# Moving small work between engines in a four-layer convolution stack: broadcast columns, pooling sums, replicas and a rectifier

## The chip, the cores and the metric

One core of a Trainium2 chip runs the whole kernel in one launch. The metric is the device time of that launch in microseconds. The engines are named as in the profile: PE (TensorE; PEld is its weight load), DVE (VectorE), ACT (ScalarE), POOL (GpSimd) and SP (SyncE, which issues all DMAs here).

## The reference

The input x is (32, 128, 56, 56) in float32: 32 images, 128 channels, 56 x 56 points (L = 3136). Four residual layers follow each other, `x = x + layer(_gn(x))`, where `_gn` is a group norm with 32 groups of 4 channels.

```python
# layer 0: mixes 4 expert matrices by attention on the pooled input, then dilated depthwise convs
attn = softmax((relu(pooled @ fc1_w.T + fc1_b) @ fc2_w.T + fc2_b) / 34.0)
y    = einsum(agg(attn, dw_weight), x) + attn @ dw_bias
out  = sum(silu(depthwise3x3(y, ds_weight, dilation=d) + ds_bias) for d in (1, 3, 5))
# layer 1: a cubic B-spline of every element, 10 coefficients
# layer 2: linear attention; q and k come from x pooled to 8 x 8 cells (7 x 7 points each)
out  = depthwise3x3(linear_attention(relu(pool @ Wq.T + bq), relu(pool @ Wk.T + bk), Wv x + bv))
# layer 3: mamba over the 3136 points, 256 inner channels, 16 states each
xn   = layer_norm_over_channels(x)
xc   = silu(conv_b + causal_conv4(in_proj_x(xn)));  z = in_proj_z(xn)
dt, B, C = split(x_proj(xc))
delta = softplus(dt_proj(dt) + dt_proj_b)
h[t] = exp(delta[t] * A) * h[t-1] + delta[t] * B[t] * xc[t]
out  = out_proj((sum_n h[t, n] * C[t, n] + xc * D) * silu(z))
```

## The kernel before

Channels are partitions, points are the free axis. An image is cut into 7 chunks of 448 points (8 rows of 56). The kernel runs layer 3 of image b while layers 1 and 2 of image b + 1 and layer 0 of image b + 2 run beside it. The program has a part before the first scan (the first images' early layers), a hardware loop over 30 images that is unrolled by 6, and two images after it.

The layer-3 scan sets the beat. A chunk has 16 steps (`STEPS`), 3584 over all images. One step covers 32 channels x 4 states in the 128 partitions, twice, as one row of 904 elements:

- ACT makes the decays, `da = exp(A * delta)`, from `rep`, in two ops; PE spreads the rows of B over the partitions into the PSUM tile `pb`.
- DVE multiplies, `db = rep * pb` (into PSUM), and runs the scan, `h = scan(da, db)` (three buffers of h).
- POOL saves the last column (`last`) and multiplies by the rows of C, `hc = h * cb`; `cb` is a copy that ACT makes from PSUM into one of four buffers of the pool `cbp`.
- PE sums `hc` over the states into `y`.

`rep` holds delta and du = delta * xc, copied to all state groups. For that `ssm_inputs` writes both to DRAM (`flat`), and `fetch` reads them back with four different partition groups as targets.

In `ssm_inputs` softplus is made as max(v, 0) + ln(1 + exp(-|v|)), where v = dt_proj(dt) + bias: ACT writes |v| into `du` from PSUM, DVE writes max(v, 0) into `delta` from the same PSUM tile, ACT applies Exp and Ln to `du`, and POOL adds. `layer_norm` of the next chunk has its ops there too: PE centres (`ctr`) into a PSUM tile, ACT squares it (`sq`) and copies it (`cen`), PE averages, ACT makes `rstd`, POOL multiplies cen by it.

All matmul targets but `pb`, `db2` and `y` share one pool of four PSUM tiles (`mm`). `group_stats` makes the group norm's mean and rstd with a chain of ops on one element per partition: `mv`, `mg`, `dm`, `vv`, `ve`, `rs` (the last on POOL). `linear_attention` sums x over the 8 x 8 cells: first over the 7 points of a row into 448 sums (`s1`, in the tile `ws`), then over 7 rows (`s2`).

The order of all this isn't the order of the code. A planner (`Plan`) records every operation with the tiles it reads and writes, prices it (`price`), and gives it a due time counted back from its step (4 us each); to that it adds a fitted date from the table `LEAD`, by engine, output and input:

```python
for w in self.works:
    w.due += LEAD.get(w.what, 0.0)
```

It then builds the order greedily with its own clock: of an engine's operations that could start first it takes the one with the earliest due time, and it counts pool tiles as taken until their last reader. The instructions are issued in that order, so almost all of them bear the one line of `issue` (L456) in the profile, and are told apart by their tiles.

Of the kernel before, what the change touches and what calls it, by code (L numbers as in the profile page):

```python
# [37 lines left out]
KEXP = 4  # L38
# [42 lines left out]
    "gpsimd delta delta": -3.5,  # L81
    "gpsimd du delta": -20,
    "gpsimd hc h": 10,
    "gpsimd ind xt": -2.5,
    "gpsimd last h": -8.5,
    "gpsimd rep": 11.5,
    "gpsimd rep last": 8,
    "gpsimd rs ve": -87,
    "gpsimd rstd cen": -144,
    "gpsimd xn": -27,  # L90
    "gpsimd xn rstd": -55,
    "gpsimd xn xn": 3.5,
    "gpsimd xt xt": 4.5,
    "scalar aggT dwT": -0.5,
    "scalar att att": 3,
    "scalar cb mm": 0.5,
    "scalar cen mm": -1,
    "scalar da rep": 13,
    "scalar dbl mm": -20.5,
    "scalar du du": -12.5,  # L100
    "scalar du mm": -65,
    "scalar hats hats": -2,
    "scalar hats stack": 2.5,
    "scalar rstd mm": -67.5,
    "scalar rstd rstd": 1.5,
    "scalar sq mm": -17.5,
    "scalar top ab": -6.5,
    "scalar ws mm": -3.5,
    "scalar yc mm": -33,
    "sync flat delta": 15,  # L110
    "sync flat du": 7.5,
    "sync flatx xt": -114.5,
    "sync out_dram xt": 30,
    "sync padded yc": 17,
    "sync rep flat": 42,
    "sync stack flatx": -8,
    "sync stack padded": -10.5,
    "sync xt x_dram": -58,
    "tensor mm aggT": 5.5,
    "tensor mm cbT": -6.5,  # L120
    "tensor mm ctr": 2,
    "tensor mm dsT": 1.5,
    "tensor mm dtT": -5.5,
    "tensor mm fc1T": -1,
    "tensor mm gmat": -21,
    "tensor mm hid": 12,
    "tensor mm ident": -15,
    "tensor mm jmat": -1,
    "tensor mm outT": -1,
    "tensor mm winT": 1.5,  # L130
    "tensor mm wpT": -50,
    "tensor mm wqT": -1.5,
    "tensor mm ws": 6,
    "tensor mm wspl": -11,
    "tensor mm wv": 4,
    "tensor mm xprojT": -2,
    "tensor y ddiag": 4,
    "vector ab mg": 4,
    "vector ab rs": -27.5,
    "vector ab ve": 1.5,  # L140
    "vector aggT dwT": -80.5,
    "vector aggb aggb": 30.5,
    "vector aggb attb": 23,
    "vector att att": -33,
    "vector att mm": -9,
    "vector attb att": -56.5,
    "vector attr att": -93.5,
    "vector bia bia": 1.5,
    "vector bia kneg": -23,
    "vector cb mm": -4.5,  # L150
    "vector ctr ident": -36.5,
    "vector cube sq": 6,
    "vector db rep": 21,
    "vector delta mm": -10,
    "vector dm mv": -6.5,
    "vector g t": 12,
    "vector h da": -4.5,
    "vector hid mm": -1,
    "vector kb mm": 18,
    "vector mcell mg": 25,  # L160
    "vector mg mm": 14,
    "vector mv st": 5.5,
    "vector mx att": -10,
    "vector mx mx": -6.5,
    "vector nm": 13.5,
    "vector nm mg": 13.5,
    "vector pooled dm": 3.5,
    "vector rden mm": 4.5,
    "vector rden rden": 0.5,
    "vector scl mm": -4.5,  # L170
    "vector sz sz": -11,
    "vector sz t": 3,
    "vector ve mm": 4,
    "vector vv dm": 1.5,
    "vector ws": 5,
    "vector ws mm": 1.5,
    "vector ws ws": 6.5,
    "vector ws xt": -36.5,
    "vector xt mm": 19,
    "vector xt xt": 6,  # L180
# [21 lines left out]
class Plan:  # L202
# [6 lines left out]
    RATE, LANDING = 2e5, 1.8  # L209
# [64 lines left out]
    def price(self, w, engine, method, args, kw):  # L274

        n = args[0].free_size()
        if method == "dma_start":
            w.cost += 0.4 if bass.MemoryType.DRAM in (args[0].space, args[1].space) else 0.6
# [202 lines left out]
def tile_conv_stack(ctx: ExitStack, tc: tile.TileContext, out: bass.AP, x: bass.AP, w: dict):  # L481
# [14 lines left out]
    cbp = pool("cbp", 4)  # L496
# [192 lines left out]
    flats = [dramp.tile([2, DI * P * CH], F32, name=f"flat{k}") for k in range(2)]  # L689
# [14 lines left out]
    plan.pitch |= {fl[:].tensor.name: DI * P * CH for fl in flats}  # L704
# [20 lines left out]
    def group_stats(st):  # L725
# [10 lines left out]
        nc.vector.scalar_tensor_tensor(vv[:], dm[:], dm[:, 0:1], mv[:, 1:2], ALU.mult, ALU.add)  # L736
# [56 lines left out]
    def dynamic_conv(xt, st):  # L793
# [18 lines left out]
        nc.vector.tensor_scalar(att[:], att[:], mx[:, 0:1], 1.0 / TEMP, ALU.subtract, ALU.mult)  # L812
        nc.scalar.activation(att[:], att[:], AF.Exp)
        nc.vector.tensor_reduce(mx[:], att[:], AX.X, ALU.add)
        nc.vector.reciprocal(mx[:], mx[:])
        nc.vector.tensor_scalar_mul(att[:], att[:], mx[:, 0:1])
# [3 lines left out]
        nc.vector.tensor_scalar_mul(attr[:], att[:], rs[:, 0:1])  # L820
# [144 lines left out]
    def linear_attention(xt, st):  # L965
# [17 lines left out]
        nc.vector.tensor_reduce(s1, xt[:].rearrange("p (a b) -> p a b", b=W // GRID), AX.X, ALU.add)  # L983
# [7 lines left out]
        nc.vector.tensor_scalar(s2, s2, mcell[:, 0:1], rs[:, 0:1], ALU.subtract, ALU.mult)  # L991
# [134 lines left out]
    def ssm_inputs(xt, k, norm):  # L1126
# [30 lines left out]
        for t, src in enumerate((delta, du)):  # L1157
            nc.sync.dma_start(flats[k % 2][t : t + 1, :].rearrange("a (d p c) -> p (a d) c", d=DI, p=P), src[:])
# [371 lines left out]
```

## Time and profile before

| | us |
|---|---|
| median of 3 runs | 14950.99 (14941.11 to 14951.97) |
| the profiled execution | 14946.83 |
| its span, first to last instruction | 14945.0 |
| DVE / POOL / ACT busy | 13958.2 / 11265.0 / 10743.3 |
| PE busy (modelled ends) | 13091.0 |
| mean granted PE clock | 0.942 |

The lines of the groups give, for an engine, an operation and its tiles: the count, the busy time, the mean of one in ns, the engine's idle time before them and what ended it. The windows view gives the busy time of each engine in a stretch of the span.

### The profile page before, as it was taken

To read this page: it belongs to the slowest core of one execution; us is meant where nothing else is said; L and a number is where in the kernel's file an instruction comes from. 1 tells how busy PE (TensorE), PEld (TensorE's weight loads), DVE (VectorE), ACT (ScalarE), POOL (GpSimd) and SP (SyncE) were. 2 spreads that over 40 slices of the span, in tenths; PEclk is the share of its full clock that TensorE was granted. 3 is DMA by queue.
4 is the path that set the end of the run, shared out by engine and by line. 5 is a ranking of instruction groups with operands and counts; after the bars stand their busy time and mean duration, and the time that the engine had idled before them with its cause. 6 is when DMAs were issued, how large, how long until landed. Compare 5 with 4: busy or idle time off the path is not lost. (4 is left out here: it accounts for less than half of the span.)

```text
span 14945.0 us, 207438 instructions
## 1 busy us (share of the span) xinstructions
PE 13091.0 (88%) x68640; PEld 4525.0 (30%) x68640; DVE 13958.2 (93%) x13510; ACT 10743.3 (72%) x17159; POOL 11265.0 (75%) x9926
## 2 busy tenths in 40 slices
PE   6888898888898888988888988889988889888887
PEld 2323333323333233333333332333332333333222
DVE  2899999999999999999999999999999999999899
ACT  3777677777777776777777777767777777777664
POOL 2777777777778777777777777777877777777776
PEclk8999999999999999999999999999999999999998
DMA  6666676666676666666666666667666667666543
GB/s 160 145 155 159 151 164 158 148 152 154 156 159 154 155 152 148 161 158 150 156 158 150 157 153 154 156 150 162 159 151 150 155 151 168 153 152 159 134 105 71
DMA packets 1326438, 2257.40 MB, mean 151 GB/s; under 512 B 143222, under 2 KB 951545, under 8 KB 1324667
## 3 DMA queue, kind: packets, MB, share of 16 engines
q1 hardware_dynamic: 1325338, 2243.87, 65.1%
q8 instruction: 553, 9.06, 0.3%
q14 instruction: 547, 4.47, 0.1%
HBM read 1813.23 MB, written 430.08 MB: 150 GB/s over the span
## 5 line engine op out<-in xcount | busy, mean ns | idle before, releaser
L456 POOL TENSOR_TENSOR hc<-h,cb 128x896 f32<-128x896 f32 x3584 | 7498.9, 2096 | 782.0 <-PE y L456 395.7
L456 DVE TENSOR_TENSOR_SCAN h<-da,db 128x904 f32<-128x904 f32 x3584 | 7279.8, 2031 | 176.8 <-ACT da L456 8.4
L456 ACT ACTIVATE da<-rep,alog 128x448 f32<-128x448 f32 x7168 | 4432.7, 663 | 2275.2 <-DVE h L456 1922.3
L456 DVE TENSOR_TENSOR db<-rep,pb 128x904 f32<-128x904 f32 x3584 | 3940.2, 1099 | 196.7 <-PE pb L456 85.5
L456 PE MATMUL pb<-dbl,sel 128*128 128x452 f32 x3584 | 1954.3, 629 | 674.5 <-DVE db L456 645.1
L456 POOL COPY last<-h 128x2 f32<-128x2 f32 x3072 | 575.6, 189 | 2308.5 <-DVE h L456 2059.2
L456 PE MATMUL y<-hc,ids 128*32 128x448 f32 x14336 | 1962.7, 573 | 177.3 <-POOL hc L456 114.3
L456 PE MATMUL mm<-stack,dsT 96*32 96x448 f32 (+1 forms) x16128 | 1819.0, 562 | 44.7 <-DMA stack<-onesd 21.2
L456 PE MATMUL mm<-xn,winT 128*128 128x448 f32 x3584 | 1619.4, 572 | 122.4 <-DVE g L456 49.7
L456 ACT ACTIVATE hats<-stack,bia 128x448 f32<-128x448 f32 x2688 | 1638.4, 663 | 4.1 <-DMA stack<-flatx 3.6
L456 PE MATMUL mm<-hats,wspl 128*32 128x448 f32 x12544 | 1423.8, 579 | 91.1 <-DVE xt L456 52.7
L456 ACT ACTIVATE hats<-hats,one,scl 128x1344 f32<-128x1344 f32 x896 | 1347.7, 1504 | 1.2
L456 ACT ACTIVATE t<-mm 128x448 f32<-128x448 f32 x1568 | 837.4, 537 | 615.9 <-PE mm L456 549.0
L456 PEld LDWEIGHTS pb<-dbl,sel 128*128 128x128 f32 x3584 | 592.3, 199 | 1828.0 <-DVE db L456 1491.6
L456 PE MATMUL mm<-dbl,sel 128*128 128x448 f32 x1792 | 883.8, 584 | 112.6 <-DVE delta L456 48.1
L456 POOL TENSOR_TENSOR xt<-xt,g 128x448 f32<-128x448 f32 x672 | 766.0, 1140 | 270.8 <-DVE g L456 239.1
L456 PEld LDWEIGHTS mm<-xn,winT 128*128 128x128 f32 x3584 | 665.7, 196 | 887.7 <-issue 718.2
L456 PEld LDWEIGHTS mm<-stack,dsT 96*32 96x32 f32 (+1 forms) x16128 | 446.4, 111 | 1227.2 <-issue 1014.0
L456 PEld LDWEIGHTS y<-hc,ids 128*32 128x32 f32 x14336 | 371.5, 111 | 1395.2 <-issue 543.0
L456 PEld LDWEIGHTS mm<-hats,wspl 128*32 128x32 f32 x12544 | 379.8, 116 | 1087.7 <-issue 664.8
L456 ACT ACT_TABLE_LOAD x512 | 656.9, 1283 | 8.7
L456 ACT COPY cb<-mm 128x448 f32<-128x448 f32 x896 | 470.3, 526 | 232.5 <-POOL hc L456 112.1
(186 smaller groups left out, 15286.5 us busy)
## 6 DMA issues: line engine op xcount, KB each, us to landing
rep<-flat SPq DMA_DIRECT2D x3584, 224.0 KB
stack<-padded SPq DMA_DIRECT2D x2688, 264.0 KB
stack<-flatx SPq DMA_DIRECT2D x896, 224.0 KB
flat<-delta SPq DMA_DIRECT2D x224, 448.0 KB
flat<-du SPq DMA_DIRECT2D x224, 448.0 KB
padded<-yc SPq DMA_DIRECT2D x224, 264.0 KB
padded<-yc SPq DMA_DIRECT2D x256, 231.0 KB
xt<-x_dram SPq DMA_DIRECT2D x224, 224.0 KB
```

The source lines that it names most:

```text
L456: call()
```

## The change

- In `group_stats`, the softmax of `dynamic_conv` and the cells of `linear_attention`, DVE ops that take a per-partition scalar column become ops of two tensors, with the column broadcast along the free axis. `vv` and the normalising of the cells become two ops each; the softmax's factor 1/TEMP moves into ACT's Exp.
- The first pooling sum (7 points of a row) becomes six additions on POOL.
- `delta`, max(v, 0), is made by ACT's Relu with the bias column.
- `flat` is laid out so that a fetch takes four transfers of 8 x 448 rows per partition, not eight of 4 x 448.
- `cbp` gets a fifth buffer, the planner's price of a DMA and its bandwidth figure change (no DMA here reaches the size of the new price), and the table `LEAD` is new throughout.

```diff
 LEAD = {
...
-    "gpsimd hc h": 10,
+    "gpsimd hc h": 10.5,
...
+    "gpsimd ws ws": 13,
+    "gpsimd ws xt": -4.5,
...
-    "scalar cen mm": -1,
+    "scalar cen mm": 172,
...
+    "scalar delta mm": -2,
...
-    "sync rep flat": 42,
+    "sync rep flat": 61,
...
-    "vector h da": -4.5,
+    "vector h da": -76,
...
-    RATE, LANDING = 2e5, 1.8
+    RATE, LANDING = 2.4e5, 1.8
...
-            w.cost += 0.4 if bass.MemoryType.DRAM in (args[0].space, args[1].space) else 0.6
+            w.cost += 0.4 if args[0].partition_size() * n < P * P * 32 else 1.0
...
-    cbp = pool("cbp", 4)
+    cbp = pool("cbp", 5)
...
-    flats = [dramp.tile([2, DI * P * CH], F32, name=f"flat{k}") for k in range(2)]
+    flats = [dramp.tile([DI, 2 * P * CH], F32, name=f"flat{k}") for k in range(2)]
...
-        nc.vector.scalar_tensor_tensor(vv[:], dm[:], dm[:, 0:1], mv[:, 1:2], ALU.mult, ALU.add)
+        nc.vector.tensor_mul(vv[:], dm[:], dm[:])
+        nc.vector.tensor_add(vv[:], vv[:], mv[:, 1:2])
...
-        nc.vector.tensor_scalar(att[:], att[:], mx[:, 0:1], 1.0 / TEMP, ALU.subtract, ALU.mult)
-        nc.scalar.activation(att[:], att[:], AF.Exp)
+        nc.vector.tensor_sub(att[:], att[:], mx[:].to_broadcast([P, KEXP]))
+        nc.scalar.activation(att[:], att[:], AF.Exp, scale=1.0 / TEMP)
...
-        nc.vector.tensor_scalar_mul(att[:], att[:], mx[:, 0:1])
+        nc.vector.tensor_mul(att[:], att[:], mx[:].to_broadcast([P, KEXP]))
...
-        nc.vector.tensor_scalar_mul(attr[:], att[:], rs[:, 0:1])
+        nc.vector.tensor_mul(attr[:], att[:], rs[:].to_broadcast([P, KEXP]))
...
-        nc.vector.tensor_reduce(s1, xt[:].rearrange("p (a b) -> p a b", b=W // GRID), AX.X, ALU.add)
+        cells = xt[:].rearrange("p (a b) -> p a b", b=W // GRID)
+        nc.gpsimd.tensor_add(s1, cells[:, :, 0], cells[:, :, 1])
+        for i in range(2, W // GRID):
+            nc.gpsimd.tensor_add(s1, s1, cells[:, :, i])
...
-        nc.vector.tensor_scalar(s2, s2, mcell[:, 0:1], rs[:, 0:1], ALU.subtract, ALU.mult)
+        nc.vector.tensor_sub(s2, s2, mcell[:].to_broadcast([P, P2]))
+        nc.vector.tensor_mul(s2, s2, rs[:].to_broadcast([P, P2]))
...
-            nc.vector.tensor_scalar(delta[:, db, :], ps, dtb[:, db : db + 1], 0.0, ALU.add, ALU.max)
+            nc.scalar.activation(delta[:, db, :], ps, AF.Relu, bias=dtb[:, db : db + 1])
...
-            nc.sync.dma_start(flats[k % 2][t : t + 1, :].rearrange("a (d p c) -> p (a d) c", d=DI, p=P), src[:])
+            half = flats[k % 2][:, t * P * CH : (t + 1) * P * CH]
+            nc.sync.dma_start(half.rearrange("d (p c) -> p d c", p=P), src[:])
...
-        flat = flats[k % 2][:, db * P * CH : (db + 1) * P * CH].rearrange("t (r q c) -> q t r c", r=NS, q=Q)
+        flat = flats[k % 2][db : db + 1, :].rearrange("a (r q c) -> q (a r) c", q=Q, c=CH)
...
-                for t in range(2):
-                    nc.sync.dma_start(reps[db][Q * s : Q * s + Q, t, :, NGRP:], flat[:, t, :, :])
+                rows = reps[db][Q * s : Q * s + Q].rearrange("p t r c -> p (t r) c")
+                nc.sync.dma_start(rows[:, :, NGRP:], flat)
```

More of the change, by code (lines that the diff above doesn't have):

```diff
@@ L80 @@
 LEAD = {
-    "gpsimd delta delta": -3.5,
-    "gpsimd du delta": -20,
-    "gpsimd hc h": 10,
[L84 to L96, printed above, removed]
-    "scalar cen mm": -1,
-    "scalar da rep": 13,
-    "scalar dbl mm": -20.5,
@@ L100 @@
[L100 to L114, printed above, removed]
-    "sync rep flat": 42,
-    "sync stack flatx": -8,
-    "sync stack padded": -10.5,
@@ L118 @@
[L118 to L121, printed above, removed]
-    "tensor mm dsT": 1.5,
[L123 to L133, printed above, removed]
-    "tensor mm wspl": -11,
-    "tensor mm wv": 4,
-    "tensor mm xprojT": -2,
@@ L137 @@
[L137 to L154, printed above, removed]
@@ L155 @@
-    "vector dm mv": -6.5,
-    "vector g t": 12,
-    "vector h da": -4.5,
[L158 to L180, printed above, removed]
+    "gpsimd delta delta": 5.5,
+    "gpsimd du delta": -35,
+    "gpsimd hc h": 10.5,
+    "gpsimd ind xt": -6,
+    "gpsimd last h": -11.5,
+    "gpsimd rep": 60.5,
+    "gpsimd rep last": 25.5,
+    "gpsimd rs ve": 10,
+    "gpsimd rstd cen": -136,
+    "gpsimd ws ws": 13,
+    "gpsimd ws xt": -4.5,
+    "gpsimd xn": -41.5,
@@ new lines @@
+    "gpsimd xn rstd": 7,
+    "gpsimd xn xn": -18.5,
+    "gpsimd xt xt": 2.5,
+    "scalar aggT dwT": 7,
+    "scalar att att": -40,
+    "scalar cb mm": -9.5,
+    "scalar cen mm": 172,
+    "scalar da rep": 13,
+    "scalar dbl mm": -3,
+    "scalar delta mm": -2,
+    "scalar du mm": -66.5,
+    "scalar hats hats": -1,
+    "scalar rstd mm": 10.5,
+    "scalar rstd rstd": -28,
+    "scalar sq mm": -8,
+    "scalar t mm": -7.5,
+    "scalar top ab": 18,
+    "scalar ws mm": -19.5,
+    "scalar yc mm": -39,
@@ new lines @@
+    "sync flat delta": -7,
+    "sync flat du": 16,
+    "sync flatx xt": -59.5,
+    "sync out_dram xt": 9,
+    "sync padded yc": -14,
+    "sync rep flat": 61,
+    "sync stack flatx": -7,
+    "sync stack padded": -14.5,
+    "sync xt x_dram": -1,
+    "tensor mm aggT": 9,
+    "tensor mm cbT": -19,
+    "tensor mm ctr": -6,
+    "tensor mm dsT": 1.5,
+    "tensor mm fc1T": -63.5,
+    "tensor mm gmat": 0.5,
+    "tensor mm ident": -111.5,
+    "tensor mm jmat": -13,
+    "tensor mm outT": -1.5,
@@ new lines @@
+    "tensor mm winT": -1.5,
+    "tensor mm wpT": 6.5,
+    "tensor mm wqT": -76,
+    "tensor mm ws": -1,
+    "tensor mm wspl": -11,
+    "tensor mm wv": -33,
+    "tensor mm wzT": 20,
+    "tensor mm xprojT": -1,
+    "tensor y ddiag": 3.5,
+    "tensor y ids": -7,
+    "vector ab rs": -26.5,
+    "vector ab ve": -47,
+    "vector aggT dwT": 6.5,
+    "vector aggb aggb": 35,
+    "vector aggb attb": -5,
+    "vector att att": -235.5,
+    "vector att mm": 9.5,
+    "vector attb att": 8,
+    "vector attr att": -18,
@@ new lines @@
+    "vector bia bia": -86,
+    "vector bia kneg": -42.5,
+    "vector cb mm": -3.5,
+    "vector ctr ident": -14.5,
+    "vector cube sq": 9.5,
+    "vector db rep": 25,
+    "vector dm mv": -0.5,
+    "vector g t": 12,
+    "vector h da": -76,
+    "vector hid mm": 98.5,
+    "vector kb mm": -15,
+    "vector mg mm": 7.5,
+    "vector mv st": -32.5,
+    "vector mx att": -47.5,
+    "vector mx mx": -20.5,
+    "vector nm": 22,
+    "vector nm mg": -1.5,
+    "vector rden mm": -49.5,
+    "vector st xt": 5.5,
@@ L181 @@
+    "vector sz sz": -51.5,
+    "vector sz t": 8.5,
+    "vector ve mm": -18.5,
+    "vector vv vv": 1.5,
+    "vector ws": 5.5,
+    "vector ws mm": 0.5,
+    "vector ws ws": -5.5,
+    "vector xc t": -3,
+    "vector xt mm": -28.5,
+    "vector xt xt": -10,
 }
@@ L703, in tile_conv_stack @@
     plan.pitch |= {fx[:].tensor.name: L for fx in flatx}
-    plan.pitch |= {fl[:].tensor.name: DI * P * CH for fl in flats}
+    plan.pitch |= {fl[:].tensor.name: 2 * P * CH for fl in flats}
     nc = plan
```

## The prediction

> **What bounds the kernel now.** I read the totals first, then the stages of one image, then VectorE's rows, then who waits. The page:
>
> ```profile
> PE 13091.0 (88%) x68640; PEld 4525.0 (30%) x68640; DVE 13958.2 (93%) x13510; ACT 10743.3 (72%) x17159; POOL 11265.0 (75%) x9926
> ```
>
> The windows view splits this run into the part before the first scan (0 to 434), the loop, and the tail, and then one image of the loop into its seven chunks. Columns: length, busy time of PE, weight loads, DVE, ACT, POOL, granted clock, DMA share, GB/s.
>
> ```profile
> 0.00:434.00 434.00, 291.50 (x1848) 104.98 (x1848) 113.69 (x336) 159.36 (x240) 97.50 (x94) 0.80 0.62 149
> 434.00:14078.00 13644.00, 12131.53 (x64299) 4194.42 (x64299) 13052.39 (x12530) 10053.88 (x16073) 10557.19 (x9296) 0.95 0.67 155
> ...
> 4076.00:4143.00 67.00, 51.90 (x238) 16.79 (x238) 64.99 (x67) 52.72 (x82) 49.95 (x47) 0.87 0.42 107
> 4143.00:4206.00 63.00, 59.31 (x344) 19.70 (x343) 60.74 (x55) 58.66 (x95) 54.70 (x50) 0.97 0.83 187
> 4206.00:4267.00 61.00, 55.65 (x311) 18.36 (x313) 58.60 (x52) 57.04 (x89) 54.09 (x52) 0.94 0.73 163
> 4267.00:4337.00 70.00, 64.26 (x379) 20.76 (x375) 69.02 (x70) 47.74 (x79) 58.40 (x53) 1.00 0.68 152
> sum 451.00, PE 403.66 PEld 138.25 DVE 435.64 ACT 335.82 POOL 352.01; mean PE 57.67 PEld 19.75 DVE 62.23 ACT 47.98 POOL 50.29
> ```
>
> In the loop VectorE is busy 95.7%, in the fourth chunk 98.6%. A chunk is as long as VectorE's work in it, so work taken off VectorE counts nearly in full there. VectorE's idle time before the loop, 320 us, is latency and is not for sale. The cover is thin, though: ScalarE is at 93% in chunks 2 and 3, TensorE at 89% over the image.
>
> VectorE's rows by form (busy us, mean ns | idle before, released by), then two of the other engines:
>
> ```profile
> L456 DVE TENSOR_SCALAR delta<-mm,dtb 128x448 f32<-128x448 f32 x448 | 299.3, 675 | 74.0 <-ACT du L456 66.6 <-PE mm L456 3.6
> L456 DVE SCALAR_TENSOR_TENSOR vv<-dm,mv 128x1 f32<-128x1 f32 x128 | 109.3, 854 | 0.3
> L456 DVE TENSOR_REDUCE ws<-xt 128x448 f32<-128x3136 f32 x32 | 108.7, 3396 | 0.0
> L456 DVE TENSOR_SCALAR ws<-ws,mcell,rs 128x64 f32<-128x64 f32 x32 | 41.4, 1294 | 0.1
> ...
> L456 POOL TENSOR_TENSOR xt<-xt,g 128x448 f32<-128x448 f32 x672 | 766.0, 1140 | 270.8 <-DVE g L456 239.1 <-DVE att L456 5.5 <-DVE pooled L456 5.3
> ...
> L456 ACT ACTIVATE du<-mm,dtb 128x448 f32<-128x448 f32 x448 | 276.9, 629 | 59.2 <-DVE delta L456 45.0 <-PE mm L456 7.7
> ```
>
> The tiny ops are the surprise: one element per partition in 854 ns. The view of the tile dm shows why:
>
> ```profile
> L456 DVE TENSOR_TENSOR dm<-mv,mg x128: 132/149/1255, 28.7 to 14452.4; 128x1 f32<-128x1 f32 x128
> L456 DVE SCALAR_TENSOR_TENSOR vv<-dm,mv x128: 185/1126/1737, 28.9 to 14455.5; 128x1 f32<-128x1 f32 x128
> L456 DVE TENSOR_TENSOR pooled<-dm,rs x32: 153/1971/1984, 32.4 to 13654.3; 128x1 f32<-128x1 f32 x32
> ```
>
> Minimum, median and maximum lie far apart. All three read two tensors in SBUF, and in the timeline a long one ends just when GpSimd's running hc, delta or xt op ends. So such an op waits for GpSimd's two-input op, recorded as busy. The heavy ops (the scan, db, g) read one operand from PSUM and don't spread.
>
> **The change, part by part** (signs are for VectorE's time).
>
> *Delta.* 448 ops of 675 ns leave: -299.3. The 74.0 of idle before them goes too where nothing else was late; the next op often needs the same producers, so I take half: -37 (0 to -74). ScalarE gets 448 ops like its du row, 629 ns, 282 us in all; over the image that is 9 us beside some 115 idle. What it costs where the cover is thin comes below.
>
> *Pooling sums.* 32 reduces of 3396 ns leave: -108.7. GpSimd gets six additions of 448 elements: by its xt row 6 x 1.14 = 6.86 us per image. They read every seventh element; no row shows that stride, so 6.86 is the near value, and twice that the far end. The sums come 3.5 us later to the attention behind them; VectorE's idle before the ops that take attention's first products (ws, kb, rden) is 14 us in all 32 images, so that costs nothing yet. But hc is queued behind these additions on GpSimd, and the scan waits for hc when h's buffers are full.
>
> *Broadcast columns.* The fused vv (854 ns) becomes a product and a sum, both with two SBUF inputs. The product inherits the wait: 0.66 + 0.13 = 0.80. The sum costs 0.15 plus a second wait between none and 0.94 (vv's median less its minimum); I take dm's mean excess, 0.18, as the op nearest in kind: 128 x (0.80 + 0.33) = 144 for 109.3, so +35 (+12 to +132). The pooled cells' op (1294 ns) becomes two likewise: +10 (0 to +35). The softmax's scalars keep the same wait in another form, and the scale moves into an Exp that runs anyway: 0, at best -3.
>
> *Replicas.* Eight transfers of 224 KB become four of 448; bytes and 1792-byte rows stay. On SP eight issues took 6.86 us in the timeline of its queue; some 1792 issues leave, and what stands behind them (stack loads, stores) goes out 3 us earlier. VectorE's db waited for replicas only 4.4 us in all, so I book 0; a worse spread of a transfer over the queues could cost some us at a chunk's start, a better one gains nothing.
>
> *Fifth cb buffer, new dates.* ScalarE's cb waited 112 us for GpSimd's hc; the buffer can take that away, but VectorE isn't behind it: 0. The built order keeps the old pattern, most work standing one to three steps earlier. I book 0 for it, -100 to +100, a sixth of the loop's VectorE idle.
>
> *Sum.* -299.3 - 108.7 + 35 + 10 - 3 = -366. Recorded ops overlap: by count times mean VectorE's rows make 460.9 us per image, its busy time is 435.6, so times 0.945: -346; with the idle 37: -383. Some 3% of it lies ahead of the loop, where it shortens nothing: -372.
>
> *Given back.* Counting rows in the built order, all six additions stand in the fourth chunk, four of them with no hc between. GpSimd there has 58.4 + 6.9 = 65.3 us of work, while VectorE's falls to about 64. With three h buffers one step of lag is hidden, so I charge 2 us per image (0 to 6). In the second chunk ScalarE rises to some 62 us by the same count, as much as VectorE keeps: 0.5 (0 to 2). 32 x 2.5 = 80. So -372 + 80 = -292: span 14,653. The profiled run had 1.8 us outside the span, and the median stands 4.2 above that run: **14,659**.
>
> Two rules bear on the moves. The Trainium skill, page "GPSIMD Engine Reference", section "Engine selection", advises VectorE for elementwise work and against GpSimd, about twice as slow on two inputs. This trace agrees on the price and says that the place decides: 6.86 us on an engine with 100 idle per image against 3.40 on one with 15; by the rule one would keep the reduce, and the gain would be some 100 us smaller. The page "ScalarE: Activation LUTs", section "Rules for kernel authors", puts relu and max on VectorE rather than ScalarE; here 675 ns against 629 differs from it, and by the rule delta would bring nothing.
>
> **Rivals.**
>
> *Neighbours take over.* If hc's delay behind the additions costs the full 6 us, ScalarE's 2 in chunk 2 come on top, and the second waits of vv and the cells are at their far ends (+122 more), -372 + 115 + 256 = 0: 14,950, no change; with half of each about 14,800. For it: GpSimd's fourth chunk. Against: the fifth chunk has 14 us of GpSimd idle to catch up in.
>
> *TensorE becomes the bound (slower).* New dates put cen, which frees one of four PSUM tiles, about seven steps behind sq in four of seven chunks (before: none or one). Some 27 tiles pass per chunk, 12 in seven steps. If each waits for one eviction (537 ns, the tanh row), that is 6.4 us per chunk; TensorE's idle in chunks 2 to 4 is 3.7, 5.4 and 5.7. That alone makes them 4.4 longer together, and the other four chunks gain 1.7 each: 14,945 - 32 x 2.4 = 14,868. But a waiting TensorE loses clock, as in chunk 1 (0.87). At 0.90, 0.88 and 0.94 there the three chunks become 70.3, 65.8 and 74.8 (59.3 x 0.97/0.90 + 6.4, and so on), +16.9 per image, less the 6.8: +323, **15,270**. It decides once stalls pass about 5 us per chunk. For it: weight loads already waited for cen 140 times, 113.6 us in all. Against: the order was made with the tile counted as taken.
>
> *The change doesn't do what it says:* if two-input ops now meet GpSimd at every turn, only the broadcast part fails, within the first rival's range.
>
> **How the numbers follow.** Forecast (VectorE stays the bound): 0.70, own range 14,450 to 14,850 (the sum with 100 for order and most of the 74 idle below; half the give-back above). Neighbours: 0.13, of which 0.05 within the bound of no change. TensorE: 0.17. I count 0.2% (30 us) as what a measurement can tell from none. Faster 0.70 + 0.08 = 0.78, same 0.05, slower 0.17. The range takes in the neighbours and the mild end of TensorE's case: 14,450 to 14,980.
>
> **What would show it.** Right: VectorE's busy time near 13,600 and still over 94% of the loop; delta in ScalarE's rows near 629 ns; six GpSimd additions near 1.14 us; vv's sum at 0.2 to 0.5 us; a fourth chunk of about 66. Wrong: VectorE's idle in the loop clearly over 660 us, released by pb or by h's buffers; a fourth chunk unchanged; a clock below 0.94; strided additions near 2 us; vv's two ops over 2 us together.

## The result: slower by 1.5%, and the profile after

The changed kernel takes 15,180.8 us (median of 4 runs, 15,108.3 to 15,211.3) against 14,951.5 for the kernel before on the same chip: 1.0148 times as long, 95% interval 1.0112 to 1.0184. The forecast was 14,659 us, with 14,450 to 14,980 as its range: the kernel became slower instead of faster, and the time lies above the range. The four runs go with the granted clock of TensorE: 0.943 in the one of 15,108 us, 0.933 in the one of 15,211. The profiled execution took 15,176.0 us, its span is 15,174.2.

The page's busy times:

```profile
PE 13118.5 (86%) x68640; PEld 4577.0 (30%) x68640; DVE 13786.1 (91%) x13190; ACT 10944.0 (72%) x17607; POOL 11502.5 (76%) x10118
```

VectorE (DVE) lost 172 us of work, where 346 were expected, and yet the span grew by 229: its idle time in the loop rose from 592 to 967 us. The windows view has the loop first, then the first five chunks of one image (columns as in the prediction):

```profile
441.00:14303.00 13862.00, 12155.45 (x64303) 4243.62 (x64302) 12894.92 (x12221) 10239.83 (x16492) 10778.73 (x9478) 0.94 0.67 152
...
4119.00:4189.00 70.00, 55.00 (x254) 20.30 (x250) 68.13 (x70) 56.71 (x90) 51.09 (x48) 0.88 0.54 128
4189.00:4249.00 60.00, 56.15 (x339) 19.76 (x340) 58.42 (x52) 57.22 (x92) 54.16 (x49) 1.00 0.80 181
4249.00:4310.00 61.00, 54.97 (x347) 18.47 (x349) 58.34 (x51) 57.09 (x92) 53.51 (x51) 1.00 0.77 169
4310.00:4377.00 67.00, 59.37 (x312) 20.59 (x304) 61.92 (x64) 49.57 (x81) 59.67 (x55) 0.95 0.64 140
4377.00:4454.00 77.00, 75.99 (x354) 26.05 (x354) 59.58 (x54) 40.45 (x69) 50.47 (x47) 0.82 0.63 147
```

The fifth chunk of the same image before, which the prediction did not show:

```profile
4337.00:4395.00 58.00, 55.15 (x287) 20.70 (x282) 55.95 (x48) 39.28 (x67) 43.67 (x41) 0.94 0.60 148
```

The fourth chunk did what was forecast (70 to 67). The fifth went from 58 to 77 us: VectorE has 60 us of work in it, TensorE (PE) is busy 76 of 77, at a granted clock of 0.82. This image is the longest of its kind. Six images earlier the unrolled loop issues the same instructions in the same order for this chunk, and there it takes 66 us at full clock:

```profile
1618.00:1684.00 66.00, 63.44 (x354) 22.83 (x346) 58.84 (x54) 40.01 (x69) 50.24 (x46) 1.00 0.73 171
```

Over 20 alike images of the loop (of six unrolled ones all but the first and the last) the fifth chunk is 71.2 us after, 58.5 before (+12.7), the other six together 6.7 shorter. So the loss has one address: the chunk in which layer 2's pooled attention runs beside the scan. Its length goes with the time for which TensorE is granted half its clock in it: 66.6 us in the three images with none, 70.4 with 10.2 us of it, 73.4 with 17.1, 77.4 with 27.3. The 12.7 us are 3.6 of work that the new dates moved into this chunk (VectorE is busy 59.7 us, 56.0 before), about 4.8 of idle time that is there at full clock too (7.2 in those three images, 2.4 before), and 4.3 of idle time that comes with the half clock (11.5 on the average).

VectorE's, ScalarE's and GpSimd's rows that answer to those of before:

```profile
L453 DVE TENSOR_TENSOR vv<-dm 128x1 f32<-128x1 f32 x128 | 115.5, 903 | 0.3
L453 DVE TENSOR_TENSOR dm<-mv,mg 128x1 f32<-128x1 f32 x128 | 104.3, 815 | 0.3
L453 DVE TENSOR_TENSOR vv<-vv,mv 128x1 f32<-128x1 f32 x128 | 56.5, 441 | 0.3
L453 DVE TENSOR_TENSOR attr<-att,rs 128x4 f32<-128x4 f32 x32 | 55.9, 1746 | 1.1
L453 DVE TENSOR_SCALAR rden<-mm 128x8 f32<-128x8 f32 x32 | 5.3, 167 | 89.4 <-PE mm L453 89.4
...
L453 ACT ACTIVATE delta<-mm,dtb 128x448 f32<-128x448 f32 x448 | 280.0, 631 | 0.0
...
L453 POOL TENSOR_TENSOR ws<-ws,xt 128x448 f32<-128x448 f32 x160 | 217.7, 1361 | 0.2
```

Delta costs ScalarE 631 ns (629 forecast). The strided additions take 1.22 us once and 1.36 five times, 8.0 us per image (6.86 forecast, 13.7 the far end). The small ops that wait for GpSimd have grown: dm (one element per partition) from 309 ns to 815, attr (four) from 238 to 1746, ctr (128) from 262 to 1720; pooled fell from 1545 to 311. The rows of dm, vv, pooled, att, attr, ctr and the cells together: 308 us before, 492 after.

What happens in the fifth chunk, by the timeline of VectorE around kb, in an image of 73.4 us:

```profile
4863.07 2.04 DVE L453 TENSOR_TENSOR_SCAN h<-da,db 128x904 f32<-128x904 f32 x1
4865.02 0.14 DVE L453 COPY kb<-mm 64x16 f32<-64x16 f32 x1
4867.39 0.17 DVE L453 TENSOR_SCALAR rden<-mm 128x8 f32<-128x8 f32 x1 [2.23 <-PE mm L453]
4867.59 0.20 DVE L453 RECIPROCAL rden<-rden 128x8 f32<-128x8 f32 x1
4870.69 1.10 DVE L453 TENSOR_TENSOR db<-rep,pb 128x904 f32<-128x904 f32 x1 [2.90 <-PE pb L453]
...
4880.86 0.62 DVE L453 SCALAR_TENSOR_TENSOR g<-t,mm 128x448 f32<-128x448 f32 x1 [3.58 <-ACT t L453]
```

and of TensorE:

```profile
4856.81 0.92 PE L453 MATMUL pb<-dbl,sel 128*128 128x452 f32 x2
...
4865.22 2.13 PE L453 MATMUL mm<-kb,ws 64*128 64x1 f32 x16 [0.61 <-DVE kb L453]
4867.28 1.57 PE L453 MATMUL mm<-xt,ws 128*64 128x392 f32 x2
4868.78 1.88 PE L453 MATMUL pb<-dbl,sel 128*128 128x452 f32 x2
4870.58 1.57 PE L453 MATMUL mm<-xt,ws 128*64 128x392 f32 x2
```

The windows view has the clock for it, before and behind the time 4867:

```profile
4859.00:4867.00 8.00, 7.27 (x67) 4.27 (x65) 5.89 (x5) 3.58 (x7) 8.00 (x8) 0.99 0.71 188
4867.00:4880.00 13.00, 13.00 (x30) 3.03 (x30) 6.65 (x6) 4.04 (x7) 8.11 (x7) 0.50 0.22 63
```

VectorE stands three times within 16 us (2.2, 2.9 and 3.6 us), each time with the next scan queued behind the waiting op. TensorE's queue has pb behind the one-column products of kb and a head product, and from 4867 to 4880 it runs at half clock: the pb pair takes 1.88 us, where the one 12 us earlier took 0.92. In the kernel before pb stood ahead of those products, and rden two scans behind kb:

```profile
4801.30 1.48 PE L456 MATMUL pb<-dbl,sel 128*128 128x452 f32 x2
4802.71 3.57 PE L456 MATMUL mm<-kb,ws 64*128 64x1 f32 x16
```

### The profile page after: what moved, and what is told of

The parts are those of the page before. It is cut to its first block, busy times and chain, and to the rows that moved or that the text cites. A ratio compares the mean times of both kernels' runs of the same rounds, so it can differ in the third digit from the quotient of the medians.

```text
span 15174.2 us, 205543 instructions
## 1 busy us (share of the span) xinstructions
PE 13118.5 (86%) x68640; PEld 4577.0 (30%) x68640; DVE 13786.1 (91%) x13190; ACT 10944.0 (72%) x17607; POOL 11502.5 (76%) x10118
## 5 line engine op out<-in xcount | busy, mean ns | idle before, releaser
L453 PE MATMUL pb<-dbl,sel 128*128 128x452 f32 x3584 | 1888.7, 610 | 623.2 <-DVE db L453 617.3
L453 PE MATMUL y<-hc,ids 128*32 128x448 f32 x14336 | 2027.5, 582 | 143.5 <-POOL hc L453 139.8
L453 PE MATMUL mm<-stack,dsT 96*32 96x448 f32 (+1 forms) x16128 | 1857.9, 564 | 174.2 <-DVE sz L453 67.1
L453 PE MATMUL mm<-xn,winT 128*128 128x448 f32 x3584 | 1659.7, 580 | 46.5 <-POOL xn L453 23.1
L453 PE MATMUL mm<-hats,wspl 128*32 128x448 f32 x12544 | 1384.3, 554 | 143.0 <-DVE sz L453 91.9
L453 PEld LDWEIGHTS y<-hc,ids 128*32 128x32 f32 x14336 | 407.7, 111 | 1356.8 <-POOL hc L453 567.6
```

The source lines that it names most:

```text
L453: call()
```

## Experiments

**Method: the order frozen.** Every edit to an operation makes the planner find another order, so an edit alone mixes two changes. In most of the runs an operation is planned as it stands, and another is issued in its place:

```diff
+    @contextmanager
+    def instead(self, *calls):
...
+        n = len(self.works)
+        yield
+        for w in self.works[n:-1]:
+            w.calls = []
+        self.works[-1].calls = [partial(getattr(getattr(self.nc, e), m), *a, **k) for e, m, a, k in calls]
```

All other instructions then stand in the same sequence on every engine. An image has 112 steps, and its fifth chunk is steps 64 to 79. "Chunk" below is the mean over the same 20 images of the one profiled execution; each ratio is to the kernel before on the same chip.

**1. Order and operations apart.** The old order with the four new parts in place of the old operations, and the new order with the old operations (five cb buffers in it).

> All new operations (delta on ScalarE, six additions on GpSimd, broadcast columns, four transfers) issued in the places that the old order gives to what they replace; the dates and the four cb buffers are the old ones. Theory O (the new order costs, the operations gain): 14,600 to 14,800, the fifth chunk of an image near 58 us as before. Theory P (the operations themselves cost, through waits of two-input VectorE ops for GpSimd and hc queued behind the additions): 15,050 to 15,250.

> The new order, issued with the old operations in it (delta and the pooling reduce on VectorE, fused scalar columns, eight transfers); the fifth cb buffer stays, since the order counts on it. Theory O: 15,350 to 15,600, the fifth chunk 70 us or more. Theory P: 14,900 to 15,050.

Measured: 15,121 us (1.0115, 1.0098 to 1.0131) and 15,340 us (1.0264, 1.0247 to 1.0281). Theory O holds for the order, in its direction and in the fifth chunk, and theory P for the operations. The new order with the old operations costs 390 us, and the new operations in it bring 159. With the old operations the fifth chunk is 71.9 us already, the image 463.1 (452.4 before).

The other way round the same sum looks different: in the old order the new operations cost 171, and the new order on top of them only 60. So the price of the order depends on the operations that stand in it. Each mixed kernel also has operations in places that were made for others: with the old operations, TensorE's weight loads wait 533 us for VectorE's delta (198 before). What holds either way is the fifth chunk: the new order makes it longer by 13.4 us with the old operations (58.5 to 71.9) and by 12.0 with the new ones (59.2 to 71.2). With the new operations, the order also takes the fourth chunk from 76.9 back to 66.4 us.

**2. The four parts, each alone in the old order.** Delta, for instance:

```diff
-            nc.vector.tensor_scalar(delta[:, db, :], ps, dtb[:, db : db + 1], 0.0, ALU.add, ALU.max)
+            relu = ("scalar", "activation", (delta[:, db, :], ps, AF.Relu), dict(bias=dtb[:, db : db + 1]))
+            with plan.instead(relu):
+                nc.vector.tensor_scalar(delta[:, db, :], ps, dtb[:, db : db + 1], 0.0, ALU.add, ALU.max)
```

> The old order, with delta alone moved to ScalarE in its old place. VectorE loses 448 ops of 675 ns and up to 74 us of waits: theory O 14,620 to 14,720 (-230 to -330). Theory P: if ScalarE's place in the queue is the cost, 14,900 or more.

14,880 us (0.9953, 0.9936 to 0.997): -69, between the two theories. VectorE's busy time falls by 235 us, but its idle time in the whole span rises by 174, from 987 to 1161. The rows of the gates in this run:

```profile
L465 DVE SCALAR_TENSOR_TENSOR g<-t,mm 128x448 f32<-128x448 f32 x672 | 410.3, 611 | 287.3 <-ACT t L465 222.1 <-POOL xn L465 65.2
...
L465 DVE SCALAR_TENSOR_TENSOR sz<-t,mm 128x448 f32<-128x448 f32 x448 | 272.7, 609 | 85.5 <-ACT t L465 84.9
```

Before, these two waited 183.6 and 6.0 us, so the gates take up all of the new idle time. They wait for tanh (`t`) in ScalarE's queue. The rectifier itself runs in only 14 us of these waits; tanh, da, hats and du run in most of them. That its 282 us make this queue late as a whole fits this and was not tested apart.

The pooling sums:

```diff
+        adds = [("gpsimd", "tensor_add", (s1, cells[:, :, 0], cells[:, :, 1]), {})]
+        adds += [("gpsimd", "tensor_add", (s1, s1, cells[:, :, i]), {}) for i in range(2, W // GRID)]
+        with plan.instead(*adds):
```

> The old order, with the first pooling sum alone made by six additions on GpSimd, all six in the reduce's old place. The three parts of the old order with all new operations were +171; delta alone was -69 and the broadcast +76, so if parts add up, this one with the transfers is about +160. Theory H (hc waits behind the additions, VectorE's scan waits for h's buffers): 15,080 to 15,130, with the fourth chunk near 77 us and VectorE idle there. Theory L (the lost time is VectorE's, by more waits of two-input ops for GpSimd): 14,950 to 15,000, and the fourth chunk near 71.

15,107 us (1.011, 1.0093 to 1.0127): +166. VectorE's second reduce stands directly behind the place that the first had:

```profile
L465 DVE TENSOR_REDUCE ws<-ws 128x64 f32<-128x448 f32 x32 | 30.6, 957 | 228.2 <-POOL ws L465 228.2
L465 DVE TENSOR_SCALAR ve<-mm 128x1 f32<-128x1 f32 x128 | 18.8, 147 | 96.5 <-PE mm L465 96.5
```

It waits 7.1 us per image for the additions, ve after it 3.0 for a matmul (0.4 before), and the fourth chunk goes from 71.0 to 78.0 us. So theory H has the time and the chunk, but not the wait: the scan's idle time is 176.3 us, as before (176.8), and none of it to speak of is for hc. In the changed kernel this reduce waits 2.9 us in all: there it stands later.

The other two take the columns and the transfers from the diff of the change in the same way, for instance:

```diff
+        two = [("vector", "tensor_mul", (vv[:], dm[:], dm[:]), {}), ("vector", "tensor_add", (vv[:], vv[:], mv[:, 1:2]), {})]
+        with plan.instead(*two):
```

> The old order, with the broadcast columns alone (vv and the pooled cells as two ops each, softmax columns broadcast). My sum had +45 us on VectorE, so 14,980 to 15,020 by theory O. Theory P (each new two-input op meets a running GpSimd op): +150 to +250, so 15,100 to 15,200.

> The old order, with four transfers of 448 KB for each fetch in place of eight of 224 KB. I booked 0: 14,930 to 14,970. If larger transfers land later than the first use, idle of db or da at the chunks' starts and 15,000 or more.

Broadcast columns: 15,025 us (1.005, 1.0033 to 1.0067): +76. VectorE's work grows by 37 us; the fifth chunk goes from 58.5 to 60.6, with 14.0 us at half clock in its first eight steps (8.5 before). It is 58.1 to 59.0 us in twelve of the 20 images and 64.2 in the eight that have 23.9 us of half clock, so this part of the price, 2.1 us per image, comes with the clock. Four transfers: 14,921 us (0.9987, 0.9977 to 0.9996): -21. The four parts add up to +152 against +171 together.

**3. Which dates?** The changed kernel, planned anew with the old dates for the attention's operations (wqT, wv, ws, kb, rden, yc).

```diff
-    "tensor mm wqT": -76,
...
+    "tensor mm wqT": -1.5,
...
-    "vector kb mm": -15,
+    "vector kb mm": 18,
```

> The changed kernel, ordered anew with the old dates for linear attention's matmuls and their evictions alone. Theory D (the fifth chunk's 71 us come from attention's new dates, which bunch its matmuls ahead of pb): 14,850 to 15,000, fifth chunk near 60. Theory G (the bunching follows from the sums coming later from GpSimd, whatever the dates): 15,120 to 15,220.

15,268 us (1.0218, 1.0201 to 1.0235): worse, and above both theories. The fifth chunk falls to 68.8, the sixth rises from 67.6 to 71.1. A date taken back among others that were fitted with the new ones is not the old order.

**4. The clock.** Three wide matmuls per image, into columns that nobody reads, among the one-column products of kb; same order.

```diff
+            with plan.instead(*([filler, one_call] if h in FILL else [one_call])):
+                nc.tensor.matmul(*real, start=True, stop=True)
```

> The changed kernel, with three matmuls of 128x128 weights by 448 columns added before the first, fourth and seventh of attention's eight one-column products; they write PSUM columns that nobody reads, so this is pure extra load on TensorE, 3 x 0.85 us per image. Theory C (the stretch is long because TensorE's clock falls to half there for 14 us, for want of load): the dip shortens, fifth chunk 64 to 67, total 15,000 to 15,100. Theory Q (the queue's order alone): +2 us per image, 15,220 to 15,260.

15,141 us (1.0138, 1.0121 to 1.0155): -40, which lies within the scatter of the changed kernel's own runs. Half clock in steps 64 to 72 falls from 10.8 to 3.4 us per image, the fifth chunk from 71.2 to 69.8. But the three matmuls have a price of their own: in images without half clock the chunk is 68.7 us with them and 66.6 without. So this run understates the clock. The images of the changed kernel alone, with the same instructions, show its part: 71.2 on the average against 66.6 without half clock, 4.6 of the 12.7 us.

**5. The places in the queues.** In the changed order, beside the attention, each pb goes directly behind the last thing that it waits for, and rden behind the next scan.

```diff
+            for i in [i for i in out[n : n + 75] if works[i].what == "tensor pb sel"]:
+                p = out.index(i)
+                q = max(k for k in range(max(0, p - 150), p) if i in works[out[k]].next)
+                out.insert(max(q, n) + 1, out.pop(p))
```

> The changed kernel with its order edited in one place: behind kb in attention, each pb is issued as soon as the db before it has read the old one (so the first stands ahead of the eight one-column products), and rden with its reciprocal stands behind the next scan. Nothing else moves. Theory Q (the fifth chunk is long because VectorE's queue waits there for rden's products and for pb behind attention's matmuls): some 5 us per image, 15,000 to 15,060, fifth chunk 65 to 67. Theory W (the matmul work in that stretch is the bound whatever its order): 15,150 to 15,210.

15,073 us (1.0083, 1.0066 to 1.01): -108. The fifth chunk is 67.3, its half clock 3.2 us. The wait for rden is gone and the one for pb behind it has fallen from 79 to 35 us in all; g's at step 72 has grown from 32 to 78. In images without half clock the chunk is 66.7 us, 66.6 before this edit. So at full clock the wait only moved, and what the edit gained goes with the half clock. Next the layer-0 convolution that feeds this g was closed ahead of kb, and g was put behind a scan:

```diff
+            for i in taps[-1:]:
+                out.remove(i)
+                out.insert(out.index(taps[-2]) + 1, i)
...
+                    out.insert(scan, out.pop(p))
```

> The changed kernel with the order edited around the pooled attention: as in the run with pb first (15,073 us), and besides the layer-0 depthwise block that the new dates split across the attention (two of its three groups of taps ahead of kb, the third behind the heads) is closed ahead of kb, and its gate g on DVE goes behind the next scan. In the run with pb first g at step 72 waits 78.2 us in all for ACT's t, which waits for the third group of taps. Theory O (what is left of the order's price in the fifth chunk is again DVE's queue standing behind a late step of PE): the wait goes, the fifth chunk falls from 67.3 us to 64.5 to 66, the kernel to 15,000 to 15,045. Rival P (PE simply has too much work in the fifth chunk: 72 + 72 depthwise matmuls there against 48 + 34.5 in the kernel before): the wait turns up at the next pb or xt, the fifth chunk stays within 0.5 us of 67.3 and the kernel within 15,055 to 15,090.

15,059 us (1.0083, 1.0066 to 1.01): nothing gained; the fifth chunk stays at 67.4. g's wait is gone, and VectorE waits 58.9 us for pb at step 72. That is what the rival said: TensorE has too much to do there. The count speaks for it: the new order puts 144 depthwise matmuls into the fifth chunk, the old one 82. The next two runs left some out, 32 and 64 of the 144, with the convolutions incomplete:

```diff
+            for b in (taps[:3], taps[3:]):
...
+                works[b[1]].calls, works[b[2]].calls = [], []
```

> The kernel of after_gate_behind, with the second and third group of taps left out of the two layer-0 depthwise blocks that stand beside the pooled attention, in five images of six (32 of 144 depthwise matmuls of the fifth chunk; the convolution is then incomplete there). All else, the order too, is the same. In the trace of after_gate_behind PE is busy 24.62 of 26 and 30.00 of 30 us in this stretch, at a clock of 0.93 and 1.00, and eight such matmuls take 0.96 us. Theory P (PE's load in the fifth chunk bounds it): up to 3.8 us an image go, the fifth chunk falls from 67.4 to 63.5 to 65.5 us, the kernel from 15,059 to 14,960 to 15,015. Rival (DVE's queue waits for the place of single steps, not for PE's amount of work): fifth chunk above 66.7, kernel above 15,040.

> As after_taps_left_out, and also two of three groups of taps left out of the first two layer-2 depthwise blocks behind the attention: 64 of the 144 depthwise matmuls of the fifth chunk, which leaves 80, about the 82 that the kernel before has there. Theory P: the fifth chunk falls to 60 to 62.5 us, near what DVE is busy in it (62.2 us with overlaps, 58.2 in the kernel before), the kernel to 14,880 to 14,950. Rival: above 65.5 us, and above 15,020.

15,062 us (1.0086, 1.0069 to 1.0103) and 15,079 us (1.0095, 1.0078 to 1.0112), fifth chunk 66.8 both times. The amount of TensorE's work is hardly it either. With less of it the half clock in steps 64 to 80 went from 2.4 to 4.6 and 5.0 us, which hides a little: in images with 3.4 us of half clock the chunk is 67.6 with all matmuls, 66.3 and 66.4 with fewer, so some 1.2 us of it are the amount. The largest single wait is again the one for pb at step 72 (79.4 and 65.0 us). The last run gave db and pb the earliest places that they can have (with the edits of part 6):

```diff
+                out.insert(max(q, scan) + 1, out.pop(p))
+                p = out.index(pb)
+                q = max(k for k in range(p - 400, p) if pb in works[out[k]].next)
+                out.insert(q + 1, out.pop(p))
```

> The kernel of after_lockfree_order with one more edit of the order beside the attention: each db of DVE goes to directly behind the scan before it, where what it reads is there, ahead of the small operations (rden, gates), and the next pb of PE directly behind that db. In the trace with 64 matmuls left out the chunk kept its length: the amount of PE's work is not what bounds it. What is left there waits for pb again (step 72, 72.6 us in all, after two head products that stand ahead of it on PE) and for the products and gates of the other layers. Theory Q (a ring of in-order queues: each place given to pb delays the step that stood there, and the wait moves on): the wait at step 72 shrinks, but xt, sz and g beside it grow; kernel within 40 us of 14,929. Rival (pb's place is what is left): fifth chunk from 67.6 to 65.5 or less, kernel at 14,830 to 14,880.

15,222 us (1.0188, 1.0171 to 1.0205): 293 slower than without this edit, and neither theory had it: the wait for pb at step 72 grew from 72.6 to 158.3 us in all. The fifth chunk of one image without it, and of one with it:

```profile
4314.00:4382.00 68.00, 64.05 (x355) 23.48 (x354) 59.83 (x55) 40.16 (x70) 51.43 (x48) 0.97 0.73 170
```

```profile
4860.00:4940.00 80.00, 74.18 (x355) 27.96 (x348) 59.74 (x54) 40.33 (x69) 50.99 (x47) 0.83 0.61 142
```

The count of matmuls is the same; the clock goes from 0.97 to 0.83, the half clock in steps 64 to 80 from 0.5 to 23 us, and the chunk from 67.6 to 78.6.

**6. The waits for GpSimd.** In the old order, then in the new one: dm and vv take an operand from PSUM (vv from a PSUM copy of dm), so that none of the chain reads two SBUF tensors; pooled becomes an op with a scalar column. In the old order the softmax and the cells were also cut into an odd number of columns and one; in the new order the broadcast forms of softmax and cells went back to scalar columns uncut.

```diff
-        nc.vector.tensor_sub(dm[:], mv[:, 0:1], mg[:])
...
-        nc.vector.scalar_tensor_tensor(vv[:], dm[:], dm[:, 0:1], mv[:, 1:2], ALU.mult, ALU.add)
...
+            ("vector", "tensor_sub", (dm[:], mv[:, 0:1], pm), {}),
+            ("vector", "tensor_copy", (dp, dm[:]), {}),
+            ("vector", "scalar_tensor_tensor", (vv[:], dp, dm[:, 0:1], mv[:, 1:2], ALU.mult, ALU.add), {}),
```

> The kernel before in its own order, with VectorE's tiny ops changed so that none reads two SBUF tensors or an even row of one: dm reads the mean from PSUM, vv takes dm from a PSUM column, pooled takes rstd as a scalar column, the softmax's 4 and the cells' 64 columns are split into 3 + 1 and 63 + 1. If these ops wait for GpSimd's running two-input op, their 854, 1545, 827 and 1294 ns fall to 130 to 350 and the time to 14,760 to 14,840. If the fresh scalar column is what makes them slow, vv keeps its 854 ns and the time stays at 14,930 or more.

14,842 us (0.9931, 0.9914 to 0.9948): -101, the best time of all. VectorE's busy time falls by 100 us and its idle time stays at 987. The view of the tile vv, and the rows of the cut ones:

```profile
L465 DVE SCALAR_TENSOR_TENSOR vv<-mm,dm,mv x128: 219/219/220, 29.1 to 14352.2; 128x1 f32<-128x1 f32 x128
```

```profile
L465 DVE TENSOR_SCALAR att<-att,mx 128x3 f32<-128x3 f32 x64 | 52.7, 823 | 0.5
```

vv takes 219 ns in all 128 places (185 to 1737 before), and still reads dm as a fresh scalar column, so that column is not what made it slow. In the kernel before, each of the 80 vv of over 400 ns ended 11 to 20 ns after an op of GpSimd did (hc 55 times, du 24, xt once). Cutting did not help: 823 ns for three columns, 827 for four before.

> The changed kernel in its own order, with the one-column chain of the group statistics read from PSUM (dm from the matmul's result, vv from a PSUM copy of dm) and the other five broadcast forms back to scalar columns; the order of all else is the same. In the changed kernel dm, vv (two), att, attr, pooled and the cells take 104.3 + 115.5 + 56.5 + 64.1 + 55.9 + 10.0 + 30.9 us of DVE. Theory L (their length is waiting for a GpSimd op that runs, which PSUM operands don't do): the vv chain falls to about 90 us from 276, attr to under 15, the kernel by 130 to 260 to 14,920 to 15,050. Rival W (DVE's time is then only idle elsewhere, in chunks that PE or ACT bound): under 80 us, above 15,100.

> The edits of the two other runs together. If they lie in different chunks and add up: 14,800 to 14,920, at or below the kernel before (14,943 to 14,951), and the change's remaining parts (pooling on GpSimd in the new order, delta on ACT, four transfers, five cb buffers) are then worth what the order costs. If each only shows the next wait: 14,950 to 15,020.

15,058 us (1.0075, 1.0058 to 1.0092): -123; dm and vv fall from 276 us to 67, the copy included, while attr stays at 1740 ns as a scalar-column op. With the order edits of after_gate_behind besides: 14,929 us (0.9997, 0.9987 to 1.0007), as fast as the kernel before. The two add up (-122 and -123 alone, -251 together) and take back all that the change cost. Compared like with like it is still behind: the kernel before with its own waits for GpSimd taken away takes 14,842 us, 88 less.

```diff
+        with plan.instead(("vector", "tensor_reduce", (s1, cells, AX.X, ALU.add), {})):
+            nc.gpsimd.tensor_add(s1, cells[:, :, 0], cells[:, :, 1])
```

> The changed kernel in its own order, with the first pooling sum back on VectorE as one reduce in the place of the last addition. In the old order the six additions cost +166. Theory S (there they cost because all six stand in one go ahead of a reduce that VectorE's queue holds; spread between hc as here they are nearly free): VectorE gets 109 us back, 15,240 to 15,300. Theory H (hc behind the additions costs in any order): 15,000 to 15,080.

The changed kernel with the first pooling sum back on VectorE in the same places: 15,243 us (1.0201, 1.0184 to 1.0218), 62 slower, and the fourth chunk goes from 66.4 to 68.6 us. So where the sums have time, GpSimd is the better place for them.

Last, the parts that had gained, put together.

> The kernel before in its own order, with those tiny ops, delta on ScalarE and four transfers. The parts alone: delta -69, transfers -21, tiny ops -100 to -190 expected. If they add up, 14,660 to 14,760; if VectorE's freed time turns into waits again, 14,800 or more.

The waits taken away, delta on ScalarE and four transfers, all in the old order: 14,849 us (0.9934, 0.9918 to 0.9951), no better than the first of them alone. VectorE's busy time is 238 us lower than there, its idle time 237 higher (987 to 1224): beside the other edit delta on ScalarE and the four transfers bring nothing.

The fifth chunk over these runs (20 images; half clock in steps 64 to 80):

| kernel | us | fifth chunk | VectorE idle in it | half clock | chunk in images without half clock (how many) |
|---|---|---|---|---|---|
| before | 14,951 | 58.5 | 2.4 | 8.5 | (0) |
| new order, old operations | 15,340 | 71.9 | 9.9 | 15.6 | (0) |
| changed | 15,181 | 71.2 | 11.5 | 11.6 | 66.6 (3) |
| three wide matmuls more | 15,141 | 69.8 | 10.4 | 3.4 | 68.7 (4) |
| pb first | 15,073 | 67.3 | 8.0 | 3.2 | 66.7 (6) |
| gate behind too | 15,059 | 67.4 | 8.1 | 2.4 | 66.9 (10) |
| 64 matmuls left out | 15,079 | 66.8 | 7.5 | 5.0 | (0) |
| waits for GpSimd and order edits | 14,929 | 67.6 | 7.9 | 0.5 | 67.5 (17) |
| db first too | 15,222 | 78.6 | 18.7 | 23.0 | (0) |

Down the last column the edits of places change nothing for the better: at full clock the chunk stays at 66.6 to 67.5 us, and VectorE's idle time in it at 7.2 to 7.7. What they change is how much half clock there is. VectorE's own work in this chunk is 58.2 us before and 62.2 after (recorded times added up; 56.0 and 59.7 without overlaps), with what the new dates moved there; that part is no loss, since it is missing elsewhere.

## Why the prediction was wrong

The forecast missed by some 520 us (-292 against +229). With the order put in first, 390 of these are the order and 133 the operations, which brought 159 in the new order where 292 were booked. With the operations put in first, 463 are the operations (+171 for -292) and 60 the order. The first is no truer than the second, and both terms of the sum failed; but the longer fifth chunk is the order's in both.

- **Dates and order, booked at 0 (-100 to +100): +12.0 to +13.4 us in every image's fifth chunk, 380 to 430 us over 32 images.** This is the step that failed. Over the whole kernel it comes to +390 with the old operations and +60 with the new ones, for which it also shortens the fourth chunk (the fifth cb buffer, not tried apart, is in both). The working looked at the built order and found the old pattern, most work one to three steps earlier. It did not ask which two things now stand side by side in the fifth chunk: attention's products and 144 depthwise matmuls instead of 82 on TensorE, rden, db and g behind late steps on VectorE. Nor did it ask what that does to TensorE's clock, which swings in this chunk between none and 27 us of half clock per image. The range of 100 was a sixth of VectorE's idle time in the loop, and that says nothing of idle time to come. The fifth chunk, with 14 us of GpSimd idle, was taken for the place to catch up in.
- **Delta, -320 with its idle: -69.** VectorE's 235 us did go (the row's 299, times 0.945, would be 283). But the freed time came back as 174 us of idle: the chunks are as long as VectorE's work only while nothing else is late. ScalarE's own price, 282 us, was right (280 to 282); what it delays, the gates that wait for `t`, was booked at 0.5 us per image and came to 5.7 (183 us over both rows).
- **Pooling sums, -103 with 64 given back: +166 in the old order, -62 in the new.** The additions' price was near (8.0 us for 6.86). The sentence that the later sums cost nothing yet, because the ops that take attention's products wait 14 us in all, looked past the very next reader, the second reduce on VectorE, which waited 228 us. In the built order of the change that reader stands later, so there the sign was right.
- **Broadcast columns, +40 with the overlap: +76 in the old order.** VectorE's work grew by 37 us, as booked; vv's two ops took 0.83 and 0.17 us, 1.00 where 1.13 was booked. The rest is idle time, most of it in the fifth chunk and with its half clock. In the new order vv's two take 0.90 and 0.44 us. What was missed is that the waits of all ops of this kind change with their places: the rows of dm, vv, pooled, att, attr, ctr and the cells grew by 184 us together. It is the places and not the broadcast form: with the old operations in the new order, attr takes 1739 ns and ctr 1654, about the same as with the new ones.
- **Replicas, 0: -21.** Below the 30 us that the prediction counts as noise.
- **TensorE as the bound (0.17, 15,270).** The nearest of the cases by its time and right in its sign. Its place was wrong: chunks 2 to 4 are 60.1, 61.5 and 66.4 us, none longer than before by more than 0.8, and weight loads wait 30.4 us for cen's late copy, less than the 113.6 before. So the near time is luck. Its second half, that a TensorE which loses clock takes the others along, is what happens, in the fifth chunk.
- **A slip in the sums.** The neighbours' rival with half of each price comes to about 14,760, not 14,800; nothing else rests on it.

The rule in the Trainium skill, page "GPSIMD Engine Reference", section "Engine selection", which would have kept the reduce on VectorE, is right in the old order (+166) and wrong in the new (-62): the place decides. The advice of "ScalarE: Activation LUTs", section "Rules for kernel authors", against relu on ScalarE is not borne out for this float32 op that reads PSUM (631 ns against 675, and -69 alone), but delta's gain is under a third of VectorE's freed time, and none of it is left once the waits for GpSimd are gone.

**What stays open.** Places in the queues move the fifth chunk between 66.8 and 78.6 us on the average, and the half clock goes along with it; 64 of TensorE's matmuls less move it by about 1. At full clock VectorE is still idle 5 us more per image there than before, and no edit took that away: each wait that was removed came back at the next step (rden and pb at step 70, then g at 72, then pb at 72). Which arrangement would free it was not found. Why the same instructions get the full clock in one image and half of it in another was not tested. That the attention's small steps on ScalarE and GpSimd coincide with the next chunk's layer norm (rstd, delta and du at steps 67 to 69, as before; kb at step 69, before at 67) fits the timelines, and no run separates it.

## What to carry to other kernels

A schedule that is fitted anew can be the largest change in a diff, even if it looks like a table of constants: test it apart, by keeping the order and swapping the operations in place, in both directions, since the two prices need not agree; and book its range from what it could cost, not from the idle time of today. Before you credit an edit with a gain, sort the images by the granted clock: here the same instructions took 66.6 to 77.4 us, and what edits of places gained in this chunk went with the clock, not with the waits that they removed. Work taken off the busiest engine counts only as far as no second engine is late in the same chunk; read the queue of the engine that receives it, and the next reader of what it makes. For small ops that wait for GpSimd, one operand in PSUM is worth more than another engine.

## What the runs showed of the hardware

- **Small ops of VectorE beside GpSimd.** With one operand in PSUM vv takes 219 ns every time; with all in SBUF up to 1737. An op with one tensor and a scalar column waits too: attr, four columns, 1740 ns on the mean; three columns 823. With one column it does not: pooled 189 to 215 ns in all places, in 25 of them inside a two-input op of GpSimd. The Trainium skill, page "SBUF — State Buffer", section "Who interferes with whom", has the same: an exclusive port pair, taken by ops with two SBUF inputs and by `tensor_scalar` in its two-port mode, the loser blocked for the whole instruction. The page has this for any op of GpSimd that reads SBUF; beside GpSimd's op on one tensor with scalars (ind, 1.87 us) this case shows no wait: 25 attb, with two SBUF inputs, ran inside one in 148 to 150 ns.
- **Half clock without a recorded pause.** In the fifth chunk of one image TensorE is recorded busy 75.99 of 77 us (ends of matmuls are modelled) and the granted clock is 0.82; with the same instructions in another, 63.44 of 66 and 1.00. The half clock stands beside the 32 and 16 matmuls of two and one columns, but these are there in the images at full clock too. Three wide matmuls among them go with 3.4 us of it where 10.8 were, and moving pb, with no matmul more, with 3.2. Where a few operations stand can swing it from 0.5 to 23 us in 16 steps; the fifth chunk of the changed kernel grows by about 0.4 us for each us of it.
